# Layer 1's quotients in VectorE's 32x32 blocks, and one accumulation of a step placed behind the background piece

## The chip, the cores and the metric

The kernel runs on one core of one Trainium2 chip. The metric is the device time of one execution in microseconds (us); three executions of the kernel before gave 2944.8, 2945.7 and 2946.02 us, and the median is used. One more execution was profiled. The engines are TensorE (PE, with its weight loads shown apart as PEld), VectorE (DVE), ScalarE (ACT), GpSimd (POOL) and SyncE (SP, which here only starts transfers).

## The reference

An fp32 batch of 4 images of 64x64 pixels with 64 channels goes through four attention layers, one after the other, each on all 4096 positions of its image.

- Layer 0: `energy = q k^T`, a softmax over rows, `out = gamma * attn^T v + x`.
- Layer 1, which the change is about: `theta` has 8 channels on 4096 positions, `phi` (8 channels) and `g` (32 channels) are pooled by two in both directions, so there are 1024 keys. `attn = softmax(theta phi^T)`, `attn_g = attn g` (32 channels), then a product with `w_o`, and the input is added. The softmax's quotient is a division by `z`, the sum of 1024 exponentials, for each of the 4096 queries.
- Layers 2 and 3: a group norm, `q`, `k`, `v`, softmax attention over 4096 keys with 64 channels, a projection and a residual.

## The kernel before, in words

**Foreground and background.** The attentions of layers 0, 2 and 3 are the foreground, twelve phases in all. One such attention has 128 units of 128 keys (or queries) by 1024, taken two at a time in 64 *steps* (`step`, L810). Everything else (all of layer 1, the norms, the projections) is cut into *background pieces*: generators that `yield` the place where the next piece may stand. `background(tempo, ...)` (L779) starts them for a phase, and the tempo is the credit that a step adds; a piece costs one credit. Nothing is scheduled later by a compiler: the order in which this program issues instructions is the order on each engine's queue.

**A step.** `first` of unit 2t and of unit 2t+1 (four 64x512 products each into a PSUM tile `s`, L1287, and ACT's exponential of it into a tile `p`, L1292), then the second product of a unit of two steps earlier (`then`, L1322, into `acc`), then `advance(MID)`, the place of a background piece or of an *urgent* item, then the second product of the other unit, in whose midst a `LATE` piece may stand. At the end of the step the functions in the list `later` run. `ready(place)` (L794) says whether a background piece will run at a place; a piece marked `ALONE` also stands at the place `MID` and keeps the `LATE` place of its step empty. Urgent items are the quotient (`turn`) and the last product (`last`) of an attention's chunk of 512 columns; they run at `MID` when their step has come.

**VectorE's accumulation.** In layers 2 and 3 VectorE adds every `p` into `zacc` (L1298, 128x1024), from which the softmax's sums come. For odd units the addition is put into `later`; for even units it is issued at once, so that it stands before what the step's `MID` piece gives VectorE:

```
later.append(add) if j % 2 else add()
```

**Buffers.** PSUM has two `s` tiles (L627) which both units' scores, the background's products and the sums share in turn, and four `acc` banks in turn. SBUF has 14 `p` tiles.

**The quotient that the foreground uses.** `turn_blocks` (L1303) has VectorE turn `zacc` within blocks of 32x32 (STREAM_TRANSPOSE, L1306) and sum each run of 32 (L1310); `sums` (L1236) adds the remaining partitions with four small products by 0/1 matrices `lanes` (64x16, L1241). The result has one sum for each turned row, so that the reciprocal takes 16 columns (L1249), and the numerators are turned the same way before the product.

**The quotient that layer 1 uses** (`normalise`, L1157): four products of `ones` (32 columns) with `zacc` (128x512 each, L1160) leave `z`, repeated over the 32 channels, in a PSUM tile; ACT copies it to SBUF and sums it for a range check (L1166), VectorE takes the reciprocal of all 512 columns in four pieces of 128 (L1169) and multiplies (L1171), and ACT sums the reciprocals for the check (L1173). Layer 1 has two chunks j = 0, 1 of 2048 queries for each image. For the first image (`bank` false, behind layer 0 of the second image) `z` is an `s` tile, and the piece is `ALONE`; both chunks are finished together after all scores. For the other three (`bank` true, behind a layer 2) `z` is an `acc` bank, chunk 0 is finished while chunk 1's scores go on in the `LATE` places, and chunk 1 afterwards.

Of the kernel before, what the change touches and what calls it, by code (L numbers as in the profile page):

```python
# [8 lines left out]
FP = mybir.dt.float32  # L9
I32 = mybir.dt.int32  # L10
AF = mybir.ActivationFunctionType
ALU = mybir.AluOpType
AX = mybir.AxisListType
# [584 lines left out]
def fast_path(tc: tile.TileContext, a: dict, out: bass.AP, bad, read_flag):  # L598
# [9 lines left out]
    nc = tc.nc  # L608
    x = a["x"]
    B, H, W, C = x.shape  # L610
    N = H * W
    P = 128
    W2 = W // 2
    S = N // 2
    NC = S // 512
    NB = N // P
# [3 lines left out]
    MID, ALONE, LATE, END = range(4)  # L620
# [4 lines left out]
    const, small = pool("const", 1), pool("small", 2)  # L625
# [3 lines left out]
    s_tile = lambda: ps_s.tile([P, 1024], FP, tag="s", name="s")  # L629
    acc_tile = lambda: ps_a.tile([P, 512], FP, tag="a", name="acc")  # L630
    x_tile = lambda name: x_p.tile([P, S], FP, tag="x", name=name)
    p_tile = lambda: p_p.tile([P, 1024], FP, tag="p", name="p")
    o_tile = lambda name: o_p.tile([P, 512], FP, tag=name, name=name)
    half = lambda i: slice(i * C, (i + 1) * C)
    quarter = lambda q: slice(q * 32, q * 32 + 32)
    chunk = lambda c: ds(c * 512, 512)
# [18 lines left out]
    def ctile(shape, name):  # L655
        return const.tile(shape, FP, tag=name, name=name)
# [53 lines left out]
    ident = ctile([P, P], "ident")  # L710
    make_identity(nc, ident)
    ones = ctile([P, P], "ones")
    nc.gpsimd.memset(ones, 1.0)
    lanes = ctile([P, C], "lanes")
    nc.vector.tensor_reduce(lanes[:, 0:32], ident.rearrange("p (a j) -> p j a", j=32), AX.X, ALU.add)
    nc.vector.tensor_copy(lanes[:, 32:C], lanes[:, 0:32])

    def twice(dst, src):
        for i in range(2):
# [22 lines left out]
    blocks = {n: (ctile([P, P], f"A{n}"), ctile([P, 1], f"Ab{n}")) for n in (0, 3)}  # L742
# [3 lines left out]
    rows(gamma0, a["L0_conv_gamma"])  # L746


    NCHECK = B * (NB + 2 + 2 * NC * 16)
    all_z, all_r = ctile([P, NCHECK], "all_z"), ctile([P, NCHECK], "all_r")  # L750
    checks = [0]

    def check_columns(n):
        i = checks[0]
        checks[0] += n
        return all_z[:, i : i + n], all_r[:, i : i + n]
# [16 lines left out]
    now = [0]  # L773
    due, before, urgent = {}, {}, []
    later = []
# [18 lines left out]
    def ready(place):  # L794
        at = back["at"]
        if place == LATE and back["alone"] == now[0]:
            return False
        return back["credit"] >= 1.0 and (at == place or place == MID and at == ALONE)

    def advance(place):  # L800
        if place == MID and urgent and urgent[0][0] <= now[0]:
            back["alone"] = now[0]
            urgent.pop(0)[1]()
        elif ready(place):
            if back["at"] == ALONE:
                back["alone"] = now[0]
            back["credit"] -= 1.0
            back["at"] = next(back["gen"], None)
# [251 lines left out]
    def layer1(on, st, bank):  # L1060
# [7 lines left out]
        s = s_tile()  # L1068
        for j in range(2):
            for e in range(2):  # L1070
                for i in range(2):
                    q = 2 * e + (i ^ j)
                    nc.tensor.matmul(
                        s[quarter(q), chunk(i)], wth1[half(i), quarter(q)], x1[half(i), chunk(2 * j + e)],
                        start=True, stop=True,
# [9 lines left out]
        for j in range(NC // 2):  # L1085
            yield MID
            s = s_tile()
# [12 lines left out]
        s = s_tile()  # L1100
# [7 lines left out]
        ps, accs, zaccs, os = {}, {}, {}, {}  # L1108
# [46 lines left out]
                nc.scalar.copy(os[j], acc)  # L1155

        def normalise(j):  # L1157
            z = acc_tile() if bank else s_tile()[:, 0:512]
            for q in range(4):
                nc.tensor.matmul(  # L1160
                    z[quarter(q), :], ones[:, 0:32], zaccs[j][:, q // 2, chunk(q % 2)], start=True, stop=True
                )
            del zaccs[j]
            r = o_tile("r")
            z_column, r_column = check_columns(1)
            nc.scalar.activation(r, z, AF.Copy, accum_out=z_column)  # L1166
            for i in range(4):
                yield MID
                nc.vector.reciprocal(r[:, ds(i * P, P)], r[:, ds(i * P, P)])  # L1169
            yield MID  # L1170
            nc.vector.tensor_tensor(os[j], os[j], r, ALU.mult)  # L1171
            yield MID
            nc.scalar.activation(r, r, AF.Copy, accum_out=r_column)  # L1173

        def last(j):
            s = s_tile()
# [4 lines left out]
            nc.vector.scalar_tensor_tensor(x1[:, wide(j)], s, bo1, x1[:, wide(j)], ALU.add, ALU.add)  # L1181

        def finish(j):

            if not bank:
                yield ALONE
            yield from normalise(j)
            yield MID
            yield ALONE
            last(j)  # L1190
# [45 lines left out]
    def sums(zsums):  # L1236

        s = s_tile()
        for k in range(2):
            for i in range(2):  # L1240
                nc.tensor.matmul(  # L1241
                    s[half(i), ds(k * 512, 16)], lanes[half(k), :], zsums[half(k), i * 16 : i * 16 + 16],
                    start=True, stop=True,
                )
        z_columns, r_columns = check_columns(16)
        nc.vector.tensor_reduce(
            z_columns, s.rearrange("p (k b) -> p b k", k=2)[:, 0:16, :], AX.X, ALU.add
        )
        nc.vector.reciprocal(r_columns, z_columns)  # L1249
        return z_columns, r_columns  # L1250
# [20 lines left out]
    def attention(st, last, not_before, name, final=None, spread=None):  # L1271

        q, k, v = st.pop("q"), st.pop("k"), st.pop("v")
        ps, accs, zaccs, zsums, os = {}, {}, {}, {}, {}
        pairs = NC * NB // 2  # L1280

        def first(u):
            c, j = divmod(u, NB)
            s = s_tile()
            for i in range(2):
                for e in range(2):
                    nc.tensor.matmul(  # L1287
                        s[half(e), chunk(i)], k[(j + i) % 2][half(i), ds(j // 2 * P + e * C, C)], q[half(i), chunk(c)],
                        start=True, stop=True,
                    )  # L1290
            p = ps[u] = p_tile()
            nc.scalar.activation(p, s, AF.Exp)  # L1292
            if j == 1:
                zaccs[c] = z_p.tile([P, 1024], FP, tag="zacc", name="zacc")
            if j >= 1:

                p0 = ps[u - 1] if j == 1 else zaccs[c]
                add = lambda: nc.vector.tensor_tensor(zaccs[c], p0, p, ALU.add)  # L1298
                later.append(add) if j % 2 else add()
            if j == NB - 1:  # L1300
                later.append(lambda: turn_blocks(c))

        def turn_blocks(c):  # L1303

            t = p_tile()
            nc.vector.transpose(t, zaccs.pop(c))  # L1306

            def sum_blocks():
                zsums[c] = small.tile([P, 32], FP, tag="zsums", name="zsums")
                nc.vector.tensor_reduce(zsums[c], t.rearrange("p (n k) -> p n k", k=32), AX.X, ALU.add)  # L1310

            later.append(sum_blocks)

        def then(u, within=None):
            c, j = divmod(u, NB)
            if j == 0:
                accs[c] = [acc_tile() for _ in range(2)]
            p = ps.pop(u)
            for cols in parts(within, j in (0, NB - 1)):
                for e in range(2):  # L1320
                    for i in range(2):
                        nc.tensor.matmul(  # L1322
                            accs[c][e][half(i), cols], v[half(e), j, :], p[half(e), chunk(i)][:, cols],
                            start=(j == 0), stop=(j == NB - 1),
                        )
            if c == NC - 1 and j == NB - 1 and final is not None:
                final(accs.pop(c), zsums.pop(c))
            elif j == NB - 1:
                o = os[c] = o_tile("o")
                acc = accs.pop(c)  # L1330
                nc.scalar.copy(o, acc[0])
                nc.vector.tensor_tensor(o, o, acc[1], ALU.add)
                urgent.append((now[0] + 2, lambda: os.update({c: turn(os[c], zsums.pop(c), spread)})))
                end = now[0] + (4 if spread is None else 6)
                urgent.append((end, lambda: last(c, os.pop(c))))
                if c == NC - 1:
                    urgent.append((end, lambda: st.update({name: True})))

        start = now[0]
        for t in range(pairs):  # L1340
            g = max(start + t + 2, not_before + t // 2)
            due.setdefault(g, []).extend([lambda *within, u=u: then(u, *within) for u in (2 * t, 2 * t + 1)])
        for t in range(pairs):
            step(lambda: (first(2 * t), first(2 * t + 1)))
        return 0
# [240 lines left out]
    t = s_tile()[:, 0:P]  # L1586
# [5 lines left out]
    t = s_tile()[:, 0:1]  # L1592
# [67 lines left out]
    for n, dsts in spectra:  # L1660
        w_d, u_d = a["L1_conv_w_" + n], a["L1_conv_u_" + n]
        r, d = w_d.shape
# [223 lines left out]
```

## Time and profile before

| what | value |
|---|---|
| median of the runs (lowest, highest) | 2945.7 us (2944.8, 2946.02) |
| the profiled execution's own time | 2945.29 us |
| its span, first to last instruction | 2943.1 us |
| granted TensorE clock | 0.999 |
| PE, PEld busy | 2910.0 us, 1147.8 us |
| DVE busy | 1843.0 us |
| ACT busy | 1925.2 us |

Times on a timeline are from the span's start. A line gives the start, the time until the last of its instructions ends, the engine, the source line, the operation, the tile that is written and those that are read, and how many records were merged. A product in fp32 leaves two records, so `x8` on a PE line is four products. In brackets stands the idle time before it and what ended it. A busy TensorE is not a measure of its work here, since overlapping records are joined; the distance from one line's start to the next is used instead.

### The profile page before, as it was taken

Reading aid. Unit: us, or ns where it says so; the run is one execution under the profiler, and the core shown is the slowest. Engines: PE = TensorE matmul, PEld = TensorE weight load, DVE = VectorE, ACT = ScalarE, POOL = GpSimd, SP = SyncE. Lnnn points to the kernel's source line nnn. Section 1 sums busy time; section 2 is a strip of 40 time slices with the busy share of each in tenths; the row PEclk is TensorE's granted clock in tenths of the full one; section 3 lists DMA queues with packets and bytes.
Section 4 is the critical chain, followed back from the end, with each engine's and each line's share of the span. In section 5 each row is a group of like instructions: output and inputs, shape, how many; then the busy total and the mean of one; then the engine's idle time right before and its main releaser. Section 6 shows DMA issues by size and latency. Waiting matters only on the chain.

```text
span 2943.1 us, 66611 instructions
## 1 busy us (share of the span) xinstructions
PE 2910.0 (99%) x29349; PEld 1147.8 (39%) x29349; DVE 1843.0 (63%) x2112; ACT 1925.2 (65%) x2769; POOL 33.6 (1%) x32
## 2 busy tenths in 40 slices
PE   9999999999999999999999999999999999999998
PEld 3333235333544433444443334333344344333333
DVE  1211742588731078872017888888988878878877
ACT  6877777665588866567886665555555555555554
POOL 0000000000000000000000000000000000000000
PEclk9999999999999999999999999999999999999999
DMA  2010000000001000000000000000000100000000
GB/s 38 1 30 5 1 2 13 8 5 17 8 5 30 1 5 5 20 7 17 1 1 5 5 22 6 19 5 9 5 19 6 22 5 8 6 19 5 9 5 10
DMA packets 76779, 30.12 MB, mean 10 GB/s; under 512 B 70465, under 2 KB 74561, under 8 KB 75073
## 3 DMA queue, kind: packets, MB, share of 16 engines
q1 hardware_dynamic: 74224, 25.37, 4.6%
q8 instruction: 232, 3.80, 0.5%
q10 hardware_dynamic: 2256, 0.41, 0.1%
q14 instruction: 67, 0.54, 0.1%
HBM read 4.79 MB, written 4.19 MB: 3 GB/s over the span
## 4 chain that ended last, share of the span: by engine, by line
PE 96%; DVE 2%; ACT 1%; issue 0%; DMA 0%; ACTq 0%; DVEq 0%
PE acc L1322 29%; PE s L1287 29%; PE s L994 15%; PE acc L1025 15%; PE s L1118 2%; PE acc L1144 2%; DVE zacc L1298 1%; ACT p L1124 1%; PE s L1144 1%; PE s L906 1%; PE s L1418 0%; PE s L885 0%; PE s L1179 0%; PE s L1090 0%; PE s L1438 0%
## 5 line engine op out<-in xcount | busy, mean ns | idle before, releaser
L1292 ACT ACTIVATE p<-s 128x1024 f32<-128x1024 f32 x1024 | 994.9, 1022 | 684.3 <-PE s L1287 655.6
L1298 DVE TENSOR_TENSOR zacc<-zacc,p 128x1024 f32<-128x1024 f32 x960 | 1173.6, 1222 | 288.1 <-ACT p L1292 240.5
L1322 PE MATMUL acc<-p,v 64*64 64x512 f32 (+1 forms) x8576 | 1017.8, 572 | 0.0
L1322 PEld LDWEIGHTS acc<-p,v 64*64 64x64 f32 x8576 | 347.7, 133 | 541.7 <-issue 541.7
L1025 PE MATMUL acc<-p,vs 64*64 64x512 f32 (+1 forms) x4224 | 513.3, 578 | 0.5 <-ACT vs L1014 0.5
L1004 ACT ACTIVATE p<-s 128x1024 f32<-128x1024 f32 x480 | 487.3, 1016 | 35.0 <-PE s L994 16.2
L1287 PE MATMUL s<-q,k 64*64 64x512 f32 x2048 | 499.4, 590 | 1.7 <-ACT p L1124 1.7
L994 PE MATMUL s<-xT,q 64*64 64x512 f32 x2048 | 488.5, 591 | 3.0 <-DVE v L910 0.9
L994 PE MATMUL s<-xT,q_swapped 64*64 64x512 f32 x2048 | 489.1, 591 | 0.7 <-DVE o L1153 0.7
L1287 PE MATMUL s<-q,xT 64*64 64x512 f32 x2048 | 488.8, 590 | 0.0
L1287 PE MATMUL s<-q,h_swapped 64*64 64x512 f32 x2048 | 480.2, 589 | 1.8 <-DVE mean L1354 0.5
L1287 PE MATMUL s<-q,k_swapped 64*64 64x512 f32 x2048 | 477.7, 590 | 0.1
L1006 DVE TENSOR_REDUCE all_z<-z 128x1 f32<-128x4 f32 x128 | 20.1, 157 | 624.3 <-ACT p L1004 624.0
L1025 PEld LDWEIGHTS acc<-p,vs 64*64 64x64 f32 x4224 | 186.6, 133 | 262.0 <-issue 198.6
L1014 ACT ACTIVATE vs<-v,all_r 64x64 f32<-64x64 f32 x512 | 176.8, 345 | 138.8 <-PE acc L1025 70.4
L994 PEld LDWEIGHTS s<-xT,q_swapped 64*64 64x64 f32 x2048 | 149.8, 133 | 143.7 <-issue 109.5
L1287 PEld LDWEIGHTS s<-q,k_swapped 64*64 64x64 f32 x2048 | 149.1, 133 | 135.1 <-issue 89.0
L1287 PEld LDWEIGHTS s<-q,h_swapped 64*64 64x64 f32 x2048 | 145.2, 133 | 142.4 <-issue 128.5
L1287 PEld LDWEIGHTS s<-q,xT 64*64 64x64 f32 x2048 | 145.3, 133 | 138.0 <-issue 130.2
L994 PEld LDWEIGHTS s<-xT,q 64*64 64x64 f32 x2048 | 149.1, 133 | 126.9 <-issue 95.6
L1287 PEld LDWEIGHTS s<-q,k 64*64 64x64 f32 x2048 | 150.0, 133 | 113.3 <-issue 92.0
L1124 ACT ACTIVATE p<-s 128x1024 f32<-128x1024 f32 x128 | 124.2, 1022 | 80.8 <-PE s L1118 80.8
(218 smaller groups left out, 1315.1 us busy)
## 6 DMA issues: line engine op xcount, KB each, us to landing
k_swapped<-k SPq DMA_DIRECT2D x8, 512.0 KB, 5.4
residual<-turned SPq DMA_DIRECT2D x128, 32.0 KB, 1.8
h_swapped<-xT SPq DMA_DIRECT2D x8, 512.0 KB, 5.8
out_dram<-turned SPq DMA_DIRECT2D x60, 64.0 KB, 2.0
xin<-in_x_dram SPq DMA_DIRECT2D x12, 256.0 KB, 6.6
q_swapped<-q SPq DMA_DIRECT2D x6, 512.0 KB, 5.9
pg<-pg SPq DMA_DIRECT2D x8, 128.0 KB, 2.3
xin<-in_x_dram SPq DMA_DIRECT2D x12, 64.0 KB, 2.3
```

What stands on the lines that cost most here:

```text
L906: nc.tensor.matmul(s[half(e), ds(i * 512 + k * C, C)], rhs[half(i), ds((g * 8 + k) * P + e * C, C)], w[half(i), half(i)], start=True, stop ...
L994: nc.tensor.matmul(s[half(e), chunk(i)], queries(m, i, e), k[half(i), chunk(c)], start=True, stop=True)
L1004: nc.scalar.activation(p, s, AF.Exp, accum_out=z)
L1014: nc.scalar.activation(vs[half(e), :], v[half(e), m, :], AF.Copy, scale=rz[half(e), m : m + 1])
L1025: nc.tensor.matmul(acc[c][half(i), cols], vs[half(e), :], ps[2 * t + n][half(e), chunk(i)][:, cols], start=(m == 0 and e == 0), stop=(m == ...
L1118: nc.tensor.matmul(ss[e][half(m), chunk(i)], pgs[0 if e == d else 1][r, ds(n * P + m * C, C)], th[r, chunk(i ^ j)], start=True, stop=True,)
L1124: nc.scalar.activation(pk[e], ss[e], AF.Exp)
L1144: nc.tensor.matmul(acc[quarter(q), :], g[:, k, :], ps[j, k][q // 2][:, chunk(q % 2)], start=(k == 0 or not bank), stop=(k == NK - 1 or not ...
L1287: nc.tensor.matmul(s[half(e), chunk(i)], k[(j + i) % 2][half(i), ds(j // 2 * P + e * C, C)], q[half(i), chunk(c)], start=True, stop=True,)
L1292: nc.scalar.activation(p, s, AF.Exp)
L1298: add = lambda: nc.vector.tensor_tensor(zaccs[c], p0, p, ALU.add)
L1322: nc.tensor.matmul(accs[c][e][half(i), cols], v[half(e), j, :], p[half(e), chunk(i)][:, cols], start=(j == 0), stop=(j == NB - 1),)
```

## The change

`normalise` of layer 1 now works as the foreground's quotient does. For each half e of `zacc`, VectorE turns it in 32x32 blocks into a `p` tile in one piece and sums runs of 32 in the next; then eight products of 64x16 with two forms of `lanes` add the partitions in an `s` tile, VectorE sums and inverts 16 columns and turns the numerators in the same piece; the last piece multiplies and turns back. The four products by `ones`, ACT's two passes and the reciprocals of 512 columns are gone. The piece that was `ALONE` for the first image is an ordinary `MID` piece now. `lanes` grows from 64 to 160 columns, filled by GpSimd and three reductions of VectorE at the start. The range check has 16 columns for each chunk in place of 1.

In `attention` the addition of an even unit goes to `later` too whenever an urgent item or a background piece will run at this step's `MID`.

```diff
-    lanes = ctile([P, C], "lanes")
-    nc.vector.tensor_reduce(lanes[:, 0:32], ident.rearrange("p (a j) -> p j a", j=32), AX.X, ALU.add)
-    nc.vector.tensor_copy(lanes[:, 32:C], lanes[:, 0:32])
+    lanes = ctile([P, 5 * 32], "lanes")
+    nc.gpsimd.memset(lanes, 0.0)
+    for i in (0, 1, 3):
+        nc.vector.tensor_reduce(lanes[:, i * 32 : i * 32 + 32], ident.rearrange("p (a j) -> p j a", j=32), AX.X, ALU.add)
+    both_lanes, lanes_of = lanes[:, 0:C], (lanes[:, 3 * 32 : 5 * 32], lanes[:, 2 * 32 : 4 * 32])
...
-    NCHECK = B * (NB + 2 + 2 * NC * 16)
+    NCHECK = B * (NB + 2 * 16 + 2 * NC * 16)
...
+    def urgent_now():
+        return urgent and urgent[0][0] <= now[0]
...
         def normalise(j):
-            z = acc_tile() if bank else s_tile()[:, 0:512]
-            for q in range(4):
-                nc.tensor.matmul(
-                    z[quarter(q), :], ones[:, 0:32], zaccs[j][:, q // 2, chunk(q % 2)], start=True, stop=True
-                )
+            zsums = small.tile([P, 4 * 16], FP, tag="zsums1", name="zsums1")
+            for e in range(2):
+                yield MID
+                t = p_tile()
+                nc.vector.transpose(t, zaccs[j][:, e, :])
+                yield MID
+                nc.vector.tensor_reduce(zsums[:, ds(e * 32, 32)], t.rearrange("p (n k) -> p n k", k=32), AX.X, ALU.add)
             del zaccs[j]
-            r = o_tile("r")
-            z_column, r_column = check_columns(1)
-            nc.scalar.activation(r, z, AF.Copy, accum_out=z_column)
-            for i in range(4):
-                yield MID
-                nc.vector.reciprocal(r[:, ds(i * P, P)], r[:, ds(i * P, P)])
-            yield MID
-            nc.vector.tensor_tensor(os[j], os[j], r, ALU.mult)
-            yield MID
-            nc.scalar.activation(r, r, AF.Copy, accum_out=r_column)
+            yield MID
+            s = s_tile()
+            for i in range(2):
+                for k in range(2):
+                    for e in range(2):
+                        nc.tensor.matmul(
+                            s[half(e), ds(k * 512, 16)], lanes_of[i][half(k), :], zsums[half(k), ds((2 * e + i) * 16, 16)],
+                            start=(i == 0), stop=(i == 1),
+                        )
+            z_columns, r_columns = check_columns(16)
+            nc.vector.tensor_reduce(z_columns, s.rearrange("p (k b) -> p b k", k=2)[:, 0:16, :], AX.X, ALU.add)
+            nc.vector.reciprocal(r_columns, z_columns)
+            t = o_tile("r")
+            nc.vector.transpose(t, os[j])
+            yield MID
+            blocks = t.rearrange("p (b f) -> p b f", f=32)
+            nc.vector.tensor_tensor(blocks, blocks, r_columns.unsqueeze(2).to_broadcast([P, 16, 32]), ALU.mult)
+            nc.vector.transpose(os[j], t)
...
         def finish(j):
-
-            if not bank:
-                yield ALONE
             yield from normalise(j)
...
-                later.append(add) if j % 2 else add()
+                later.append(add) if j % 2 or urgent_now() or ready(MID) else add()
```

More of the change, by code (lines that the diff above doesn't have):

```diff
@@ L798, in ready @@
         return back["credit"] >= 1.0 and (at == place or place == MID and at == ALONE)
+    def urgent_now():
+        return urgent and urgent[0][0] <= now[0]
     def advance(place):
-        if place == MID and urgent and urgent[0][0] <= now[0]:
+        if place == MID and urgent_now():
             back["alone"] = now[0]
@@ L1241, in sums @@
                 nc.tensor.matmul(
-                    s[half(i), ds(k * 512, 16)], lanes[half(k), :], zsums[half(k), i * 16 : i * 16 + 16],
+                    s[half(i), ds(k * 512, 16)], both_lanes[half(k), :], zsums[half(k), i * 16 : i * 16 + 16],
                     start=True, stop=True,
```

## The prediction

> **What bounds the kernel now.** I read the page first: the busy table and the chain that ended last.
>
> ```profile
> PE 2910.0 (99%) x29349; PEld 1147.8 (39%) x29349; DVE 1843.0 (63%) x2112; ACT 1925.2 (65%) x2769; POOL 33.6 (1%) x32
> ...
> PE 96%; DVE 2%; ACT 1%; issue 0%; DMA 0%; ACTq 0%; DVEq 0%
> ```
>
> TensorE's queue sets the end; a change counts only by the work it takes from that queue and by the time for which the queue stands still for a buffer. DVE and ACT have a third of their time free on average, which says little about single stages. Next the groups of instructions that the edit touches (busy us, mean ns):
>
> ```profile
> L1160 PE MATMUL acc<-zacc,ones 128*32 128x512 f32 x48 | 6.3, 598 | 0.0
> L1160 PE MATMUL s<-zacc,ones 128*32 128x512 f32 x16 | 2.1, 605 | 0.0
> L1241 PE MATMUL s<-zsums,lanes 64*64 64x16 f32 x256 | 9.2, 194 | 1.0 <-ACT p L1292 0.6 <-DVE zsums L1310 0.4
> L1169 DVE RECIPROCAL r<-r 128x128 f32<-128x128 f32 x32 | 29.6, 936 | 0.0
> L1306 DVE STREAM_TRANSPOSE p<-zacc 128x1024 f32<-128x1024 f32 x32 | 39.9, 1245 | 2.7
> ```
>
> Busy time misleads for TensorE, so prices come from the timeline. In the first image's stage, the starts of the second products:
>
> ```profile
> 393.36 1.04 PE L1025 MATMUL acc<-p,vs 64*64 64x512 f32 x8
> 394.33 1.07 PE L1160 MATMUL s<-zacc,ones 128*32 128x512 f32 x8
> 395.32 1.09 PE L1025 MATMUL acc<-p,vs 64*64 64x512 f32 x8
> 397.95 1.04 PE L1025 MATMUL acc<-p,vs 64*64 64x512 f32 x8
> 402.54 1.90 PE L1025 MATMUL acc<-p,vs 64*64 64x512 f32 x16
> 405.97 1.90 PE L1025 MATMUL acc<-p,vs 64*64 64x512 f32 x16
> ```
>
> A bare step takes 405.97-402.54 = 3.43; one with a `z` takes 4.59 (393.36 to 397.95, and to 402.54). In the stage of chunk 0 of the second image:
>
> ```profile
> 620.16 1.04 PE L1160 MATMUL acc<-zacc,ones 128*32 128x512 f32 x8
> ...
> 621.71 0.63 ACT L1166 ACTIVATE r<-acc 128x512 f32<-128x512 f32 x1
> ...
> 622.92 1.94 ACT L1292 ACTIVATE p<-s 128x1024 f32<-128x1024 f32 x2
> ...
> 624.30 1.73 PE L1118 MATMUL s<-th,pg 8*64 8x512 f32 x16
> ```
>
> Here ACT's pass over `z` stands ahead of the step's exponentials, and the score product of 624.30 stretches from the usual 1.11 to 1.73, waiting for them. Last, a stop that VectorE's order makes, in layer 3:
>
> ```profile
> 2561.30 2.55 DVE L1298 TENSOR_TENSOR zacc<-zacc,p 128x1024 f32<-128x1024 f32 x2
> 2561.51 0.24 PE L1353 MATMUL s<-sums,avg 64*64 64x1 f32 x8
> ...
> 2563.76 0.15 DVE L1354 TENSOR_REDUCE var<-s 128x1 f32<-128x2 f32 x1
> ...
> 2563.97 0.65 PE L1287 MATMUL s<-q,h_swapped 64*64 64x512 f32 x2 [0.45 <-DVE var L1354]
> ```
>
> TensorE had filled its `s` tile at 2561.75; VectorE emptied it at 2563.91, because a previous odd and this step's even addition stood first. With two `s` tiles the next score product could not start.
>
> **What the Trainium skill says.** "Perfetto Trace Analysis", Identifying the Most-Contended Engine: matmul busy share is no good measure of the distance to the limit. The trace agrees: 99% busy, yet steps of one content differ by 0.7. The same page, Optimizing Tensor Performance (Matmuls): independent groups should rotate through PSUM banks, so that evacuation overlaps the next product; the stop above is where two tiles don't suffice. "VectorE: DVE Perf Modes", First, the fixed hardware budget: reciprocal is an iterative divide with a repeat count of 8. The trace agrees: 936 ns for 128 columns against 1222 for an addition of 1024. The same page, The three transpose paths: VectorE turns 32x32 blocks only; 128x1024 takes 1245 ns here.
>
> **The change part by part.** The order of instructions built from both kernels moves nothing on TensorE except the `z` products and, two steps earlier, the rest of the first image's background.
>
> *First image.* Removed: two steps with 4.59-3.43 = 1.16 each, 2.3. Added: both chunks' sums fall in one piece. The stage of L1241 prices four small products: L1241 starts at 630.01 and L1322 at 630.09, 0.09 on the queue, so eight are about 0.2, twice 0.4. The second chunk needs the `s` tile of the step's second score, whose exponential in this layer ends about 3.3 into the step (405.36 to 407.53 in the step begun at 404.26), while the queue gets there at 1.71+0.86+0.2 = 2.8: a stop of 0.5. Net -1.4. No scores compete, so `ALONE` isn't missed.
>
> *Other three images, removed.* Chunk 1: L1160 at 676.95, next line at 677.94, 0.99. Chunk 0: without L1160 the next score product comes 0.86 earlier; without L1166 ACT's chain is 621.25 copy, 621.71 copy (L1331), 622.17 exponentials, ending 0.75 earlier, so the stretched score product ends 0.75 earlier. Together -1.75. ACT's second pass (L1173, 0.63+0.20) was hidden.
>
> *Added there.* Two groups of eight, +0.4. On VectorE, chunk 0's reciprocals (936 each) become turns and sums (1245, 1211) in the same four pieces, while a step with layer 1's scores lasts 5.64 (starts of L1322 at 605.13 and 610.77) and has four additions. Two on the same `zacc` start 1.33 apart (2.55 for two, less 1.22), layer 1's two 1.13 (2.35), others about 1.1: piece 1.15, additions 1.33+1.1+1.13, and 1.12 to the next piece, 5.8 a step. VectorE falls behind by 0.15 a step; before it gained (5.34, starts 639.21 and 644.55 of L1298). By hand from 630.3, when `turn`'s sums are ready: `turn` to 632.0, the two additions to 634.4, the first turn there; three rounds later the urgent `last` (L1472, before at 651.30) starts at 651.8 and frees its `s` tile at 653.1, needed at 652.7: stop 0.4. Two steps on, the sums' tile comes free some 0.2 to 0.3 after the second score half asks for it. This is `s` in place of an `acc` bank, in a step that isn't `ALONE`. Chunk 1: 1.15+1.33+1.1 = 3.6 a step against 3.43, plus the foreground's turn and sum (1245+1211) in that stretch: stop about 0.15. Sum 0.8. Behind the late operations stand only additions, whose `p` tiles come round after three steps or more. Net per image -1.75+0.4+0.8 = -0.55, for three -1.65. Unknown ends: no stops (-1.35 each), or a backlog of one more step's piece each time (+1.5 each).
>
> *The deferred addition.* A background or urgent operation no longer waits for the same step's even addition (1.1 to 1.3). Stops that this takes away, each as the distance from the score product's line to L1322's, less 1.71: 2056.28 (2.43, 0.7), 2169.27 (2.41, 0.7), 2562.49 (2.39, 0.65), 2614.93 (2.33, 0.6); behind an attention's `last`, 718.03, 1217.24 and 1716.75 (1.97, 0.25 each); and 2551.05, where L1241 waited 0.60 for an exponential queued behind ACT's square, which waited 1.57 for VectorE (L1496 at 2548.15, 1.1 earlier now): 0.7. Sum -4.1. The price: VectorE may stand idle until the piece's product is there, and both additions follow, 1.33 apart. That ends some 3.0 into the next step, whose product is ready at 3.3: no stop follows.
>
> *At nothing.* The larger `lanes`: two reductions more (372 ns each) and a GpSimd fill, done near 2.9, while VectorE's next work is at 3.96. The range check's 752 columns for 632: 0.5 more of VectorE in the last phase, under 3.43 us steps with 2.5 of additions. No transfers are added or moved past.
>
> Sum: -1.4-1.65-4.1 = -7.15 on the profiled execution's 2945.29, so 2938.1; the median stands 0.4 above it: 2938.5.
>
> **Rivals.** (1) *VectorE's queue takes it back*: in the three `bank` stages the stops are double (1.6), and half of the 4.1 returns at other places, since the additions aren't fewer. For: VectorE at 102.6 us of 128 in 552 to 680 already, and nearly 3 us added for each chunk. Against: all later work has slack. +2.4+2.05 on the forecast: 2943. (2) *No stops at all*: the `bank` stages give 1.35 each, the first image 1.9, and small stops I didn't list vanish (about 1.5): 2934. (3) *Slower*: one mechanism, the `s` tile of chunk 0's sums. VectorE reaches it behind the backlog, the queue of TensorE stands, both units' next scores are late, ACT and so the additions too. It decides where each `bank` image loses over 4.4 more than I count (13.1 in all): some 0.75 of a step of 5.64, which takes a round of 7 instead of 5.8. Then 2952. Against: turns and sums are measured at 1245 and 1211. (4) *The sums' products don't do what they should*: each column of 64x16 costs 0.09 per four in a quiet place; between other tile shapes 0.1 to 0.2 more. Inside (1).
>
> **How the numbers follow.** A difference of 0.2% (5.9 us) is about what a measurement can tell here. Forecast 52% (own range 2936 to 2941, mostly below 2939.8), rival 1 30%, rival 2 12%, rival 3 6%. Faster: 46 of the 52 and the 12, with 2 of rival 1, 60%; slower 6%; within 0.2%, 34%. For 8 in 10 I leave out the lower end of rival 2 and rival 3: 2934 to 2944.
>
> **What would show it.** Right: no L1160; PE products of 64x16 with lanes x128 more at under 0.1 us a group of four; the steps near 393 and 398 at 3.4 and one at 4.3; the stop after 2562 (then some 4 us earlier) gone; the waits "L1287 <- DVE" gone from the list. Wrong: L1118 waiting long for VectorE's reduction of the sums, score lines in the `bank` stages over 2.5 long, or ACT's exponentials waiting for additions (a `p` tile not free).

## The result and the profile after

| | kernel before | changed kernel |
|---|---|---|
| median (lowest, highest), 20 runs of each side by side | 2946.45 us (2944.8, 2947.43) | 2942.36 us (2940.77, 2943.43) |
| profiled execution, its span | 2945.29 us, 2943.1 us | 2942.18 us, 2940.4 us |
| DVE, ACT busy | 1843.0 us, 1925.2 us | 1868.2 us, 1915.3 us |

The ratio is 0.9986, with a 95% interval of 0.998 to 0.9992: a gain of 4.1 us, where the forecast had 7.15. It lies in the range (2934 to 2944), but outside the likeliest case's own range (2936 to 2941). The range holds it because it was drawn wide enough for rival 1, whose 2943 is nearer than the forecast's 2938.5. The gain stays under the 0.2% (5.9 us) that the forecast wanted for "faster", to which it had given 60%; the interval excludes no gain at all.

Lines of the changed kernel have other numbers: L1301 is the score product that was L1287, L1312 the addition L1298, L1336 the second product L1322, L1255 and L1260 the foreground's sums L1241 and L1246, L1368 the mean L1354, L1457 the values L1443, L1486 the urgent `last` L1472, L1545 and L1556 the residual. Layer 1's new quotient is L1169 (turn), L1171 (sums of runs), L1178 (eight small products), L1183 to L1186 (sum, reciprocal, turn of the numerators), L1189 and L1190 (multiply, turn back). The kernels of the experiments have numbers of their own; in their lines the operation and the tiles say what stands there.

The busy table and the groups of the changed kernel:

```profile
PE 2906.7 (99%) x29413; PEld 1145.5 (39%) x29413; DVE 1868.2 (64%) x2145; ACT 1915.3 (65%) x2737; POOL 33.8 (1%) x33
...
L1178 PE MATMUL s<-zsums,lanes 64*64 64x16 f32 x128 | 3.3, 204 | 0.5 <-ACT p L1010 0.5
L1255 PE MATMUL s<-zsums,lanes 64*64 64x16 f32 x256 | 9.1, 192 | 0.4 <-DVE zsums L1324 0.4
L1169 DVE STREAM_TRANSPOSE p<-zacc 128x1024 f32<-128x1024 f32 x16 | 19.6, 1233 | 0.0
L1171 DVE TENSOR_REDUCE zsums<-p 128x32 f32<-128x1024 f32 x16 | 19.1, 1204 | 0.0
```

Products and durations are as the working assumed. TensorE lost 3.3 us of busy time and ACT 9.9; VectorE gained 25.2. In the first image's stage, TensorE's timeline:

```profile
404.48 1.90 PE L1031 MATMUL acc<-p,vs 64*64 64x512 f32 x16
407.91 1.04 PE L1031 MATMUL acc<-p,vs 64*64 64x512 f32 x8
408.77 0.37 PE L1178 MATMUL s<-zsums,lanes 64*64 64x16 f32 x16
409.60 0.42 PE L1178 MATMUL s<-zsums,lanes 64*64 64x16 f32 x16 [0.45 <-ACT p L1010]
409.85 1.07 PE L1031 MATMUL acc<-p,vs 64*64 64x512 f32 x8
```

A bare step is 3.43 long (404.48 to 407.91); the one with both groups of sums has them in a row, and the second waits 0.45 for an exponential, where 0.5 was expected. That step costs 1.11 more than a bare one, where the working had 0.9; the two steps of 4.59 are gone. In layer 3, where TensorE used to stop after 2562:

```profile
2558.60 2.55 DVE L1312 TENSOR_TENSOR zacc<-zacc,p 128x1024 f32<-128x1024 f32 x2
2558.68 1.07 PE L1336 MATMUL acc<-p,v 64*64 64x512 f32 x8
2559.54 0.27 PE L1367 MATMUL s<-sums,avg 64*64 64x1 f32 x8
2559.63 1.10 PE L1336 MATMUL acc<-p,v 64*64 64x512 f32 x8
2560.52 0.62 PE L1301 MATMUL s<-q,xT 64*64 64x512 f32 x2
...
2561.07 0.15 DVE L1368 TENSOR_REDUCE var<-s 128x1 f32<-128x2 f32 x1
```

`var` leaves its `s` tile at 2561.22, 1.7 after its product began (before: 2561.51 to 2563.91, 2.4), and no stop follows. So far the forecast's picture. What it didn't have is in the list of TensorE's waits (total us, times, longest):

```profile
PE s L1301 <- DVE xT L1486: 1.8, 3, 0.6
...
PE s L1301 <- DVE all_z L1260: 1.5, 3, 0.5
...
PE s L1301 <- DVE all_z L1183: 0.6, 3, 0.2
```

None of the three stands in the list of before. Each comes three times, once in each later image. The first, in chunk 0 of the second image:

```profile
645.01 1.24 DVE L1169 STREAM_TRANSPOSE p<-zacc 128x1024 f32<-128x1024 f32 x1
646.17 2.51 DVE L1312 TENSOR_TENSOR zacc<-zacc,p 128x1024 f32<-128x1024 f32 x2
...
648.60 2.35 DVE L1139 TENSOR_TENSOR zacc<-zacc,p 128x1024 f32<-128x1024 f32 x2
649.31 0.62 PE L1480 MATMUL s<-residual,w 64*64 64x128 f32 x16
...
650.87 1.24 DVE L1486 SCALAR_TENSOR_TENSOR xT<-s,bp,xT 128x256 f32<-128x256 f32 x2
...
652.25 0.65 PE L1301 MATMUL s<-q,k_swapped 64*64 64x512 f32 x2 [0.61 <-DVE xT L1486]
```

VectorE goes from one line to the next without a gap. The product of 649.31 is done near 649.9, but `last` (L1486) gets its turn at 650.87, behind two pairs of additions, and the next score product has no `s` tile. The second, at the end of chunk 1:

```profile
700.03 0.69 DVE L1189 TENSOR_TENSOR r<-r,all_r 128x512 f32<-128x512 f32 x1
...
700.75 0.71 DVE L1190 STREAM_TRANSPOSE o<-r 128x512 f32<-128x512 f32 x1
701.39 2.51 DVE L1312 TENSOR_TENSOR zacc<-zacc,p 128x1024 f32<-128x1024 f32 x2
701.55 0.26 PE L1255 MATMUL s<-zsums,lanes 64*64 64x16 f32 x8
...
703.82 0.18 DVE L1260 TENSOR_REDUCE all_z<-s 128x16 f32<-128x32 f32 x1
704.04 0.25 DVE L1263 RECIPROCAL all_r<-all_z 128x16 f32<-128x16 f32 x1
704.06 0.65 PE L1301 MATMUL s<-q,k_swapped 64*64 64x512 f32 x2 [0.49 <-DVE all_z L1260]
```

Here it is the foreground's own quotient that comes late: layer 1's last piece (L1189, L1190) and the additions behind it stand ahead of the sum L1260, which follows its product by 2.27. Before, the same pair was 0.91 apart:

```profile
702.03 0.25 PE L1241 MATMUL s<-zsums,lanes 64*64 64x16 f32 x8
702.94 0.18 DVE L1246 TENSOR_REDUCE all_z<-s 128x16 f32<-128x32 f32 x1
```

To see where the time went, I took the start of each step's score products in both traces and followed how the difference changes. For the second image, times of before: the four `z` products of chunk 0 gone −0.63, those of chunk 1 −1.16; the two groups of eight small products +0.20 and +0.23; stops behind `last` +0.75, behind chunk 0's sums +0.17, behind chunk 1's sums +0.50, behind the foreground's sums +0.72, and +0.17 two steps on. Together +0.95 (the same places of the other two images give +0.91 and +0.93): each later image loses, before what the deferral gives.

By stage, with three of the experiments below (us against before; the first 30 us, where loading varies by a few tenths to some us, are left out):

| stage (times of before) | forecast | whole change | quotient alone | deferral alone | first image's quotient and deferral |
|---|---|---|---|---|---|
| first image, 380 to 545 | −1.4 | −1.32 | −1.32 | 0 | −1.31 |
| three later images, 545 to 2040 | −2.4 | +0.35 | +2.19 | −1.56 | −1.69 |
| layers 3 and 2 after them, 2040 to 2640 | −3.35 | −3.08 | −0.65 | −3.41 | −3.08 |
| sum | −7.15 | −4.05 | +0.22 | −4.97 | −6.08 |

The forecast's −2.4 is −1.65 for the quotients and three times 0.25 of the deferral. The sum of −4.05 agrees with the measured −4.1; nearly all of the miss, 2.75 of 3.1, lies in the three later images.

### The profile page after: what moved, and what is told of

Read it like the earlier page. It is cut to its first block, busy times and chain, and to the rows that moved or that the text cites. A ratio compares the mean times of both kernels' runs of the same rounds, so it can differ in the third digit from the quotient of the medians.

```text
span 2940.4 us, 66740 instructions
## 1 busy us (share of the span) xinstructions
PE 2906.7 (99%) x29413; PEld 1145.5 (39%) x29413; DVE 1868.2 (64%) x2145; ACT 1915.3 (65%) x2737; POOL 33.8 (1%) x33
## 4 chain that ended last, share of the span: by engine, by line
PE 79%; DVE 6%; issue 1%; ACT 0%; DVEq 0%
PE acc L1336 27%; PE s L1301 27%; PE acc L1031 10%; PE s L1000 9%; DVE zacc L1312 4%; PE s L1124 1%; PE acc L1150 1%; PE s L1432 0%; DVE zacc L1139 0%; PE s L912 0%; PE s L891 0%; PE s L1196 0%; DVE zsums L1171 0%; ACT p L1130 0%; PE s L1480 0%
## 5 line engine op out<-in xcount | busy, mean ns | idle before, releaser
L1312 DVE TENSOR_TENSOR zacc<-zacc,p 128x1024 f32<-128x1024 f32 x960 | 1173.5, 1222 | 181.4 <-ACT p L1306 116.6
L1336 PE MATMUL acc<-p,v 64*64 64x512 f32 (+1 forms) x8576 | 1013.4, 572 | 0.0
L1336 PEld LDWEIGHTS acc<-p,v 64*64 64x64 f32 x8576 | 349.4, 133 | 533.8 <-issue 533.8
L1301 PE MATMUL s<-q,k 64*64 64x512 f32 x2048 | 493.6, 591 | 2.1 <-ACT p L1130 2.1
L1301 PE MATMUL s<-q,xT 64*64 64x512 f32 x2048 | 490.3, 589 | 0.0
L1301 PE MATMUL s<-q,k_swapped 64*64 64x512 f32 x2048 | 479.1, 590 | 3.8 <-DVE xT L1486 1.8
L1301 PE MATMUL s<-q,h_swapped 64*64 64x512 f32 x2048 | 479.4, 589 | 0.5 <-DVE v L1457 0.2
L1031 PEld LDWEIGHTS acc<-p,vs 64*64 64x64 f32 x4224 | 180.4, 133 | 267.1 <-issue 202.4
L1301 PEld LDWEIGHTS s<-q,h_swapped 64*64 64x64 f32 x2048 | 149.9, 133 | 135.9 <-issue 127.6
L1301 PEld LDWEIGHTS s<-q,k_swapped 64*64 64x64 f32 x2048 | 146.3, 133 | 143.5 <-issue 85.1
L1301 PEld LDWEIGHTS s<-q,xT 64*64 64x64 f32 x2048 | 150.2, 133 | 133.3 <-issue 127.4
L1301 PEld LDWEIGHTS s<-q,k 64*64 64x64 f32 x2048 | 147.3, 133 | 116.2 <-issue 96.6
```

Of the source, the lines that this page charges most:

```text
L1031: nc.tensor.matmul(acc[c][half(i), cols], vs[half(e), :], ps[2 * t + n][half(e), chunk(i)][:, cols], start=(m == 0 and e == 0), stop=(m == ...
L1301: nc.tensor.matmul(s[half(e), chunk(i)], k[(j + i) % 2][half(i), ds(j // 2 * P + e * C, C)], q[half(i), chunk(c)], start=True, stop=True,)
L1336: nc.tensor.matmul(accs[c][e][half(i), cols], v[half(e), j, :], p[half(e), chunk(i)][:, cols], start=(j == 0), stop=(j == NB - 1),)
```

## The experiments

My theory after the result: *VectorE's backlog*. In the later images the new quotient costs VectorE more in each step than the step has, and the operations that free `s` tiles stand behind. Rivals: the sums' `s` tile in place of an `acc` bank; a cost spread elsewhere; and, for the deferral, other reasons why two of its sites fell short.

**One half at a time.** Without the deferral (`e1_quotients`):

```diff
-                later.append(add) if j % 2 or urgent_now() or ready(MID) else add()
+                later.append(add) if j % 2 else add()
```

> The quotients alone; even additions at once as before. Backlog theory (VectorE falls behind in the three stages where layer 1 runs behind layer 2): the first image gives 1.2, each other image loses about 1 as in the changed kernel and up to 1.3 more at each of three evacuations that now wait for one addition more: 1 to 6 us slower than before. Rival (the deferral does nothing inside those stages, it only gained in layer 3): the changed kernel plus its 2.6 of layer 3, so 1 us faster than before.

And the deferral alone (`e2_deferral`), which is the kernel before with the new condition:

> The deferred addition alone, layer 1's quotients as before. Backlog theory: it keeps the 2.6 us of layer 3 and about 0.5 us of each layer 2, some 4 us faster than before, as fast as the whole change or a little faster, since the quotients net nothing. Rival (the quotients carry the gain): under 2 us faster.

Measured: the quotient alone 2946.53 us, ratio 1.0 (0.9991 to 1.0008); the deferral alone 2941.12 us, ratio 0.9983 (0.9976 to 0.999), beside 2946.37 before. So the whole of the gain is the deferral's, and the quotient gives back in three images what it gains in the first. The medians put the deferral alone 1.2 ahead of the whole change; their intervals overlap, so that this rests on the traces (−4.97 against −4.05). In the trace of the quotient alone the stops at 706 and 699.5 are 0.79 and 0.75: the deferral makes these two smaller, not larger. The one behind `last` is 0.69 there and 0.75 in the whole change.

**Less work for VectorE in each step.** The changed kernel, with the quotient's VectorE pieces in every second step for the later images (`e3_paused`, three places):

```diff
-                yield MID
+                yield from [MID] * (1 + bank)
```

> The changed kernel with layer 1's VectorE pieces only in every second step in the three later images. Backlog theory: VectorE no longer falls behind, the stops behind the last product of layer 2, behind the sums and behind the foreground's own sums (together some 1.9 us an image) go: 4 to 6 us faster than the changed kernel, about 2937. Rival (the sums' s tile in place of an acc bank makes the stops, whatever VectorE's queue): within 1.5 us of the changed kernel.

Measured: 2936.39 us (2935.47 to 2936.84), ratio 0.9965 (0.9952 to 0.9979), an interval that lies wholly below that of the change. It is the fastest kernel of this study, 10 us ahead of before. The work is the same and only spread; the waits for L1486, L1260 and L1183 are gone from the list. Its VectorE at the place of the first stop:

```profile
646.52 2.35 DVE L1139 TENSOR_TENSOR zacc<-zacc,p 128x1024 f32<-128x1024 f32 x2
649.97 1.26 DVE L1486 SCALAR_TENSOR_TENSOR xT<-s,bp,xT 128x256 f32<-128x256 f32 x2 [1.10 <-PE s L1480]
651.13 2.54 DVE L1312 TENSOR_TENSOR zacc<-zacc,p 128x1024 f32<-128x1024 f32 x2
653.60 1.21 DVE L1171 TENSOR_REDUCE zsums<-p 128x32 f32<-128x1024 f32 x1
```

VectorE now waits 1.10 for the product, where TensorE waited for VectorE. With the backlog taken away the stops are gone, so it was their cause. The pauses have a price of their own: against the change the second and third image gain 2.3 and 2.1, the fourth only 1.1. There the background isn't done when the phase ends, and its last products (L891, L912) run between two phases, from 1794.4 to 1797.7, with a stop of 0.29 among them and one of 0.37 behind them.

**The buffer rival.** The partition sums as four 128x64 products in one `acc` bank for the later images, no `s` tile (`e4_acc`):

```diff
-            s = s_tile()
+            s = acc_tile() if bank else s_tile()[:, 0:512]
             for i in range(2):
-                for k in range(2):
-                    for e in range(2):
-                        nc.tensor.matmul(
-                            s[half(e), ds(k * 512, 16)], lanes_of[i][half(k), :], zsums[half(k), ds((2 * e + i) * 16, 16)],
-                            start=(i == 0), stop=(i == 1),
-                        )
+                for e in range(2):
+                    nc.tensor.matmul(
+                        s[half(e), 0:16], lanes_of[i], zsums[:, ds((2 * e + i) * 16, 16)], start=(i == 0), stop=(i == 1)
+                    )
             z_columns, r_columns = check_columns(16)
-            nc.vector.tensor_reduce(z_columns, s.rearrange("p (k b) -> p b k", k=2)[:, 0:16, :], AX.X, ALU.add)
+            nc.vector.tensor_copy(z_columns, s[:, 0:16])
```

> The changed kernel with the partition sums of layer 1 as four products over all 128 partitions into one acc bank in the three later images (one s tile for the first). Backlog theory: only the stops behind these sums go (0.2 and 0.4 an image, and 0.1 for each group of four products fewer), 2 to 3 us faster than the changed kernel; the stops behind the last product of layer 2 and behind the foreground's sums stay. Rival (the s tile is the cause): all of them go, 5 us or more faster.

Measured: 2943.65 us, ratio 0.9992 (0.9983 to 1.0), 1.3 slower than the change by the medians. The stops behind the sums of both chunks went (−0.50 and about −0.14), so these need the `s` tile as well as the backlog. But the one behind the foreground's sums grew (0.7 each, 2.1 in all), and `last`'s stayed at 1.8. The products themselves became dearer, which I hadn't thought of. TensorE of this kernel and then of the changed one, around chunk 0's group:

```profile
658.96 1.04 PE L1334 MATMUL acc<-p,v 64*64 64x512 f32 x8
659.93 0.41 PE L1177 MATMUL acc<-zsums,lanes 128*64 128x16 f32 x8
660.27 0.66 PE L1334 MATMUL acc<-p,v 64*64 64x256 f32 x8
```

```profile
658.80 1.04 PE L1336 MATMUL acc<-p,v 64*64 64x512 f32 x8
659.66 0.37 PE L1178 MATMUL s<-zsums,lanes 64*64 64x16 f32 x16
659.86 0.64 PE L1336 MATMUL acc<-p,v 64*64 64x256 f32 x8
```

From the second product's start to its next part it is 1.31 with four 128x64 products and 1.06 with eight 64x64 ones. As the second product's first half alone takes 0.86, that is 0.45 against 0.20. To keep this apart from the backlog, the same sums in the paused kernel (`e6_paused_acc`):

> The paused kernel (2936.4), with its partition sums as four 128x64 products, in an acc bank in the three later images. Theory (with VectorE's backlog gone the s tile of the sums costs nothing, and the four products between 64x64 ones cost some 0.25 more a group than the eight small ones): seven or eight such groups, 1.5 to 2 slower than the paused kernel, 2938. Rival (the s tile still costs a stop): equal or up to 1 faster, 2935.5 to 2936.5.

Measured: 2938.71 us (2937.47 to 2939.31), ratio 0.9972 (0.9962 to 0.9983): 2.3 slower than the paused kernel by the medians. The trace has steps of +0.27 at each of the six groups of the later images and +0.11 once in the first image's stage, where the second group waits for its tile anyway: 1.8 in all. In that stage the four products write an `s` tile, and there too they start later, 0.97 after the second product (408.35 to 409.32) where eight start after 0.86 (407.91 to 408.77). So the later start isn't due to the `acc` bank. The `s` tile has no cost that these traces show once VectorE is on time; the tile shape has.

**Where the backlog costs.** The new quotient for the first image only, the old one for the others, with the deferral (`e5_first_image`; the definition of `normalise_bank`, a copy of the old quotient, and the range check's columns are left out here):

```diff
-            yield from normalise(j)
+            yield from normalise_bank(j) if bank else normalise(j)
```

> The new quotient in the first image only; the other three images keep the old one; the addition is deferred as in the change. Theory (the new quotient gains 1.2 us in the first image and loses some 0.95 in each of the other three, by VectorE's backlog): about 1.2 us faster than the deferral alone (2941.1), so 2940, which is 2 to 3 us faster than the whole change (2942.4), and the chunk 0 and chunk 1 stops of the second image (behind L1486, L1183 and L1260 of the changed kernel) are gone. Rival (the loss is not in those three images, but spread, for instance in the larger range check or the larger lanes): as the whole change, 2942 or more.

Measured: 2940.58 us (2939.91 to 2941.2), ratio 0.998 (0.9972 to 0.9988), 1.8 ahead of the change; the three waits are gone. The table's last column has the three later images at −1.69 where the change has +0.35, which would make 0.68 for the new quotient in each. But the third image of this trace has a stop of another kind, in the middle of products of the background, that no other trace shows there:

```profile
1237.04 0.39 PE L912 MATMUL s<-wv,xT 64*64 64x64 f32 x10 [0.70 <-issue]
```

It makes its step 0.94 longer. Image by image the change is behind by 1.02, −0.03 and 1.05; without the stop the third is 0.91, and the mean 0.99, which fits the +0.95 read place by place. Whether each execution of this kernel has the stop isn't known: the medians' 1.8 is nearer to the 2.0 of the traces with it than to the 3.0 without.

Pauses in chunk 1 alone (`e7_pause_chunk1`, with `1 + (bank and j == 1)`):

> The changed kernel, with VectorE's pieces of the quotient in every second step in chunk 1 of the three later images, and in every step, as in the change, in chunk 0. Theory (each chunk makes its own backlog): chunk 1's stops (0.5 behind its sums and 0.72 behind the turn's sums) vanish, chunk 0's (0.75 and 0.37) stay: about 3 to 3.7 us faster than the whole change, some 2939, and 3 us slower than with both paused (2936.4). Rival (chunk 1 inherits a backlog that chunk 0 leaves): the stop behind the turn's sums stays above 0.4, and the time is above 2940.5.

Measured: 2938.65 us (2937.44 to 2939.63), ratio 0.9973 (0.9962 to 0.9983). The list of waits has lost L1260 and L1183; L1486's 1.9 is left. So chunk 1 makes its own backlog and doesn't inherit it. The trace shows −0.50, −0.72 and −0.17 at chunk 1's places in the second image, as listed above, and by the medians chunk 0's pauses are worth the other 2.3. The traces have only 1.5 for them (sums of −9.64 and −8.14), since the price in the fourth image falls in the kernel with both pauses.

**The pauses without the deferral** (`e9_paused_alone`):

> The new quotient with its VectorE pieces in every second step in the three later images, the even addition not deferred. Theory (the backlog is the whole loss of the new quotient): the quotient gains 1.2 in the first image and some 1.3 in each of the other three, so 5 us faster than before, 2941 to 2942, against 0.2 slower without the pauses. Rival (pauses only help together with the deferral): within 2 us of the kernel before.

Measured: 2943.87 us (2942.93 to 2944.51), ratio 0.9991 (0.9982 to 0.9999), 2.7 faster than the quotient alone and 2.7 faster than before, about half of what I expected. Neither number holds: the theory's is some 2 off, the rival's bound (within 2 us of before) 0.7. VectorE and TensorE of this kernel:

```profile
754.94 1.24 DVE L946 STREAM_TRANSPOSE xT<-xin 128x1024 f32<-128x1024 f32 x1
756.00 0.28 PE L1255 MATMUL s<-zsums,lanes 64*64 64x16 f32 x8
756.10 2.51 DVE L1312 TENSOR_TENSOR zacc<-zacc,p 128x1024 f32<-128x1024 f32 x2
758.53 0.18 DVE L1260 TENSOR_REDUCE all_z<-s 128x16 f32<-128x32 f32 x1
...
758.77 0.65 PE L1301 MATMUL s<-q,k_swapped 64*64 64x512 f32 x2 [0.73 <-DVE all_z L1260]
```

The pauses put all later background work a few steps back. Now turns of the next image's input (L946; in the fourth image a sum for layer 3's norm, L1501), which before stand some 40 us ahead of another of the foreground's quotients, run beside that quotient, and the same stop appears there: 2.2 in three images. In the paused kernel with the deferral the same sum L1260 comes at 757.82, 1.41 after its product instead of 2.53, and no stop follows; the difference of the two traces puts 0.99 on it in each image. The two measures help each other: together they gain 10.0, apart 5.2 and 2.7.

**Two sites of the deferral.** Near 2056 and 2169 it brought 0.2 to 0.6 of the expected 0.7 each; the whole change kept a stop of 0.22 and 0.23 there, the deferral alone one of 0.23 at 2169. I first thought that the addition deferred behind the urgent residual stood in the way. A kernel before in which only a background piece defers (`e8_ready_only`, without `urgent_now()`):

> The kernel before, in which the even addition is deferred only behind a background piece, not behind an urgent operation. Theory (in layers 3 and 2 the deferral brought only 0.23 of the expected 0.7 at 2056 and 2169 since the addition deferred behind the urgent residual stands ahead of the next evacuation, so that four additions lie between the two as before): here only three do, the stops of the score product near 2057 and 2170 of the kernel before (0.48 and 0.46 behind mean and v) are gone, some 0.45 more gained at each than with the whole deferral; the stops behind urgent operations (0.25 in each of three images, and whatever else) come back: 2941 to 2943 in all. Rival (the evacuation is late for another reason, the product or the semaphore path): 0.2 to 0.5 of stop stays at both places.

Measured: 2942.48 us (2940.92 to 2943.73), ratio 0.9987 (0.998 to 0.9994). The time fits, the mechanism doesn't: the step at 2169 keeps its wait of 0.23, and both steps are as long as in the deferral alone (3.56 and 3.88, there 3.57 and 3.90). That theory fell. VectorE's timeline in the deferral alone suggests why (in this kernel's numbers L1301 is the addition, L1446 the values, L1534 and L1545 the residual):

```profile
2157.73 2.54 DVE L1301 TENSOR_TENSOR zacc<-zacc,p 128x1024 f32<-128x1024 f32 x2
2160.19 1.28 DVE L1446 TENSOR_TENSOR v<-s,bv 128x512 f32<-128x512 f32 x2
2161.39 2.54 DVE L1301 TENSOR_TENSOR zacc<-zacc,p 128x1024 f32<-128x1024 f32 x2
2163.85 0.70 DVE L1534 STREAM_TRANSPOSE residual<-h_swapped 64x512 f32<-64x512 f32 x1
2164.56 0.71 DVE L1534 STREAM_TRANSPOSE residual<-xT 64x512 f32<-64x512 f32 x1
2165.30 0.69 DVE L1545 TENSOR_TENSOR turned<-turned,residual 128x512 f32<-128x512 f32 x1
2165.91 2.55 DVE L1301 TENSOR_TENSOR zacc<-zacc,p 128x1024 f32<-128x1024 f32 x2
2168.38 1.28 DVE L1446 TENSOR_TENSOR v<-s,bv 128x512 f32<-128x512 f32 x2
```

From the first `v` to the second there is no idle time, and four additions and the residual lie between them in every order. Between the two, reordering can only use up a gap: before had one of 0.33 here, at 2163.70, and one of 0.46 at 2056.39, waiting for an exponential or for the addition ahead. If this is so, less work must bring what order couldn't. In `e10_no_residual_add` the attention's result isn't added to layer 3's residual (its output lacks that part):

```diff
-            nc.vector.tensor_tensor(t, t, residual(c), ALU.add)
-            store(c, t, slice(0, 16), [nc.sync.dma_start])
+            store(c, residual(c), slice(0, 16), [nc.sync.dma_start])
```

> The deferral alone, with layer 3's residual stored without the attention's result: its addition to turned (L1545, 0.69 long, 15 times) is left out. Theory (near 2056 and 2169 VectorE works without a gap from one background evacuation to the next, so an order can't bring the second one forward, only less work can): with 0.61 less on VectorE between them, mean and v come 0.6 earlier, and the two stops of 0.23 that the deferral left there are gone. Rival (the evacuation waits for its product): mean and v come no earlier against the second products of their steps, and the stops of 0.23 stay. In time only 0.5 to 1 either way, so the trace decides.

Measured: 2941.35 us, ratio 0.9982 (0.9975 to 0.9989), in time no different from the deferral alone. In the trace no wait is left at either place, and the two steps are as long as bare ones, 3.43 and 3.44, which is 0.14 and 0.46 less than with the deferral alone and the 0.7 less than before that the forecast had. The same stretch of this kernel:

```profile
2165.14 2.55 DVE L1301 TENSOR_TENSOR zacc<-zacc,p 128x1024 f32<-128x1024 f32 x2
2167.74 1.29 DVE L1446 TENSOR_TENSOR v<-s,bv 128x512 f32<-128x512 f32 x2
```

The `v` that followed the previous one by 8.19 now does so by 7.73 (2160.01 to 2167.74), and the first score product that needs its tile doesn't wait.

## Why the prediction was right or wrong

**First image: right.** −1.4 predicted, −1.32 found, with the second group's wait of 0.45 for 0.5, and the steps of 3.43 where it said. The step with both groups is 4.54 long (4.3 was named), and small shifts in other steps make up half of that.

**Later images, removed: right.** 1.75 predicted, 0.63 + 1.16 = 1.79 found, in part by luck: the parts were 0.75 and 0.99. The 0.99 was the distance to the next line; by whole steps a `z` costs 1.16, as the working had itself measured in the first image. ACT's chain ends some 0.7 earlier, as forecast, but one reading was wrong: the score product that was to be stretched by ACT's pass over `z` is still 1.61 long without the pass (L1124 at 623.22, before 1.73), behind ACT's two copies.

**Later images, added products: right.** 0.4 predicted, 0.20 + 0.23 found. Rival 4 (the products cost more between other shapes) didn't come about; it would have for 128-row products.

**Later images, VectorE's stops: the step that failed.** The forecast had 0.8 in an image; 2.31 came. By its three terms: behind the urgent `last` 0.4, measured 0.75; behind chunk 0's sums 0.25, measured 0.17; chunk 1 0.15, measured 0.50 + 0.72 + 0.17 = 1.39. Chunk 1 was the fault. There the working set an average of 3.6 of VectorE against a step of 3.43, added the foreground's turn and sum, and called the overflow 0.15. It never walked chunk 1's queue operation by operation, as it did for chunk 0, where the walk put `last` at 651.8 and its tile free at 653.1 on before's times; with the 1.19 by which the change is ahead there, the trace has 652.1 and 653.3. The foreground's own sums, L1260, which meet layer 1's last piece, were in no term. A net of −0.55 became +0.95 in the second image; against the kernel without the new quotient there it is +0.68 on average, 0.99 without the one foreign stop. My rival 1 named this mechanism and had 1.6 of stops for it: the chosen case took the smaller size without a walk that excluded the larger.

**The deferral: right in sum, unevenly in its places.** −4.1 predicted for it, −4.97 by the trace of it alone, −5.2 by the median. The sites at 2551, 2562 and 2614 gave 0.85, 0.68 and 0.58 for 0.7, 0.65 and 0.6. Those at 2056 and 2169 gave 0.57 and 0.22 in the deferral alone, and 0.23 each in the whole change, for 0.7 each: the working took the distance to an undisturbed step as the gain, without asking whether VectorE had a gap to give. Why 2056 gave 0.57 in one kernel and 0.23 in the other stays open; the quotient alone, with no deferral, is 0.33 shorter there too. Smaller stops that it didn't list, by 0.1 to 0.3 in the later images and 0.1 in several steps of layer 3, made up for them. The second half of rival 1, that half of the deferral returns elsewhere, didn't happen: layers 3 and 2 kept 3.08 of 3.35.

**The signs it named.** L1160 gone, small products x128 more, the stop after 2562 gone: seen. "L1287 <- DVE gone from the list" was wrong: the old waits of that kind went or shrank, and three new ones came, of 3.9 in all. Of the signs against it, the long wait of L1118 (now L1124) that it watched for didn't come, nor did exponentials that wait for additions in the `bank` stages. Score lines of about 2.5 did (2.52 at 650.61, 2.44 at 702.53), but at the release of `last`'s tile and of the foreground's sums.

Left open: by how much the whole change is slower than the deferral alone. The medians say 1.2 and the traces 0.9, from one trace each, but the intervals overlap. Nor did I run a version that gives the quotient's pieces to the steps with the most room instead of to every second one.

## What to carry to other kernels

When an edit moves work from a full engine to one with a third of its time free, walk that engine's queue through the stage, instruction by instruction, past the last moved one, and find every operation on it that frees a buffer of the full engine, the foreground's own too: in chunk 1 of this kernel an average load of 1.05 (3.6 in a step of 3.43) cost 1.39 of stops where the removed products had cost 1.16. Spread the pieces until the queue has gaps again, then look what the later pieces meet. Before you price a reordering, look how long the engine idles between the two operations that stay where they are: at 2169 it idled 0.33 and the new order won 0.22, while less work won the whole 0.7.

## What the runs showed of the hardware that I had not expected

Four products of 128x64 with 16 columns, set between 64x64 ones, held TensorE's queue for 0.45 us, eight of 64x64 with the same sums for 0.20 us. The group of half as many products started 0.97 after the second product it follows, where eight 64x64 ones start 0.86 after, and took 0.34 where those take 0.20. In the paused kernel the difference was 0.27 at each of six places. The Trainium skill, "TensorEngine Tiling (Array Packing)", Key Properties, says that changing the tiling mode, not just the tile, drains TensorE; the 0.11 before the first of the four agrees with that, but which part of the 0.25 is the change and which the products was not measured apart. The products that the change removes fit the picture: four of 128x32 with 512 columns cost 1.16 a step, four of 64x64 with 512 columns 0.86.
